# Four layers on one core: D u of two images added in a transfer, the last chunks of layer 3's first part shared out anew, and the order of the scans' first pair

## The chip, the cores and the metric

The kernel runs on one core of one Trainium2 chip. The metric is device time in microseconds (us). A core has five engines that work side by side, each through its own list of instructions in order: TensorE (PE, matmul, with its weight loads as PEld), VectorE (DVE), ScalarE (ACT), GpSimd (POOL) and SyncE (SP), which here only issues transfers. Sixteen DMA engines move data between DRAM and the on-chip memory. POOL and ACT can issue transfers too. An engine waits for another, or for a transfer, by a semaphore.

## The reference

Four layers follow each other on four images of 64 x 64 pixels and 128 channels: neighbourhood attention (layer 0), full attention over 4096 pixels with a group norm (layer 1), a gated pair update with a layer norm (layer 2), and a selective scan in four directions (layer 3). The change touches layer 3:

```python
xb, z = jnp.split(x @ Win, 2, axis=-1)            # 256 channels each
xb = silu(depthwise_conv_3x3(xb, conv_w) + conv_b)
xs = jnp.stack([xf, xf[..., ::-1], xt, xt[..., ::-1]], axis=1)
x_dbl = jnp.einsum('bcl,cd->bdl', xs_flat, Wxproj)  # dt (8 rows), B, C
dt_out = jnp.einsum('kdr,kbrl->bkdl', dt_weight, dt_kb)
delta = softplus(dt_out + dbias)
xc = exp(delta * A) * xc + delta * u * B            # the scan
y  = xc * C  +  u * Dv                              # D u
y = y0 + y1 + y2 + y3                               # directions turned back
out = (layernorm(y * silu(z))) @ Wout
```

The data of the four scan directions are regrouped by a reshape: direction k of the scan takes its delta, B and C from image k, and u of image k drives the scans that end in output b = 0 to 3. What concerns the change is that D u of image i must be added to the output of all images, forwards or backwards, and turned or not. The sum over directions is kept in DRAM, in two orders t = 0 (not turned) and t = 1 (turned).

## The kernel before

The images are handled one after another. For each image layer 0 runs in blocks of 128 pixels, then layer 1 in 32 query blocks. Beside layer 1 (`between(i)`, called after block i) run two further things: layer 2 of the same image, in eight chunks of 512 pixels with four steps each (`turn`, `mix`, `add`, `norm`), and layer 3's *first part* (`front(b)`, its function `turn(i)`). The first part of image b takes chunks 4 to 7 of image b - 1 and then chunks 0 to 3 of image b. For the last image nothing follows, so its chunks 4 to 7 are done at the end, by `end(i)`, for i from 30 to 42; attention's last block is over at about i = 33.

The first part does the following with a chunk n of image i:

- `load`, `project`: 128 x 512 inputs are multiplied with `win` into x for the convolution, in `xh` (one slot for even, one for odd chunks, each with a row above and one below, which are copied between neighbouring chunks by POOL, L785 and L786). The row below a chunk is known only when the next chunk is projected.
- `gate`: z's half, silu, stored in `zf_d`.
- the convolution with nine taps. In most chunks ACT makes the first product (`begin`), ACT and POOL do four taps (`multiply`, `add_parts`: `gsum`, `tp`), and DVE four (`add_taps`, L858). At the end, PE does it for chunks 5 and 6 of the last image (`convolve_by_pe`, L873), with nine matmuls by diagonal matrices for each half f of the 256 channels. Chunk 7 gives six taps to DVE and two to POOL (`taps`).
- `activate`: silu to u. `lower`: `pd` (x_dbl), written to `dbl_d`; B as a row for every partition (`pb` by PE in chunk 3 and at the end); D u; and u times B, stored in `ub_d`.

D u is handled in `lower` in two ways. Images 0 and 2 (even) scale u on ACT (L934) and store it once, in their own output's place of `y_d` (`sum_of`). Images 1 and 3 (odd) had `load_du` load what the image before stored (L898, SP), add their own by one DVE operation (L929, written reversed), and store the result to all four outputs (L931, SP). Each half of a chunk is 256 KB.

`layer_3` then runs the scans in 64 pairs of steps. A step is 1024 pixels of one half f, one image k and one output b. For each pair: `deltas` (PE `pdt`, ACT softplus `de` L1206, POOL `inp` = de times u B, L1210), `decay` (ACT exp to `h`, L1220, in two PSUM buffers), `back` (DVE scan L1234, then times C into `yo`, L1248), and POOL issues a transfer that adds `yo` to `y_d` (L1249). `deltas` of the next pair is written ahead of `decay` of the present one. Softplus and exp need different tables on ACT. The scans use u B of half f = 0 for the first four pairs (`early.ub`, loaded ahead), then of f = 1 (`load_ub`, L1145, issued by SP in front of the first pair). A last part adds the turned sums, multiplies by the gate, norms and projects.

The order of instructions on an engine is not that of the program's text: a list scheduler at build time places them, except that instructions passed to `keep_in_program_order` keep theirs. SP's queue is such an ordered list as well; a transfer in it that has to wait holds up all behind it.

Of the kernel before, what the change touches and what calls it, by code (L numbers as in the profile page):

```python
# [22 lines left out]
F32 = mybir.dt.float32  # L23
AF = mybir.ActivationFunctionType
ALU = mybir.AluOpType
# [4 lines left out]
P = 128  # L30
B, H, W, C = 4, 64, 64, 128
L = H * W
NT = L // P
BR, BC = 8, 16
CH = 512
# [103 lines left out]
def layers_0_to_2(  # L139
# [15 lines left out]
    def ps_o(shape, name):  # L155
        return psp.tile(shape, F32, name=name, tag="o", bufs=2)
# [594 lines left out]
    def by_image_rows(t):  # L751
        return t.rearrange("p (i j) -> p i j", j=W)

    def front(b):
# [33 lines left out]
        def project_row(i, n):  # L788

# [34 lines left out]
        def taps(i, n):  # L824


            v = (1, 0) if n < NCH - 1 else (-1, 0)
            gp, ve = [v, (-1, 1), (1, -1), (1, 1)], [(-v[0], 0), (0, -1), (0, 1), (-1, -1)]
            return (gp[:2], ve + gp[2:]) if (i, n) == (B - 1, NCH - 1) else (gp, ve)

        def multiply(i, n, f, which):
            for k in which:
# [31 lines left out]
                for t in range(9):  # L864
                    nc.gpsimd.tensor_scalar(dg[:, f, t, :], ident, cc[:, f, t:t + 1], None, ALU.mult)

        def convolve_by_pe(i, n, f):
            ps = ps_o([P, CH], "pc3")
            sums.setdefault(n, []).append(ps)
            order = [(0, 0)] + [(dy, dx) for dy in (-1, 0, 1) for dx in (-1, 0, 1) if (dy, dx) != (0, 0)]  # L870
            for k, (dy, dx) in enumerate(order):
                r0, r1, c0, c1 = region(n, dy, dx)
                nc.tensor.matmul(  # L873
                    by_image_rows(ps)[:, r0:r1, c0:c1], lhsT=x_of["dg"][:, f, 3 * (dy + 1) + dx + 1, :],
                    rhs=xh[:, n & 1, f, 1 + r0 + dy:1 + r1 + dy, c0 + dx:c1 + dx], start=(k == 0), stop=(k == 8),
                )

        def activate(i, n, apart=False):
            if apart:
                u_of[i, n] = [tmp.tile([P, CH], F32, name="u1", tag="c512", bufs=9) for _ in range(2)]  # L880
                for f in range(2):
                    if (i, n) in ((B - 1, 5), (B - 1, 6)):
                        nc.scalar.activation(u_of[i, n][f], sums[n][f], AF.Silu, bias=cl("conv_b", f))
# [11 lines left out]
        def load_du(i, n):  # L895
            for f in range(2):
                z = x_of[i, n, "z", f] = tmp.tile([P, CH], F32, name="du", tag="c512", bufs=9)
                nc.sync.dma_start(z, sum_of(i, n, f, i - 1))  # L898

        def lower(i, n):  # L900


            lo, hi = CH * n, CH * n + CH
            u = u_of[i, n]
            pd = ps_t([P, P], "pd")
            for f in range(2):
                for g in range(4):
                    nc.tensor.matmul(
                        pd[HD * g:HD * g + HD, :], lhsT=wx[:, f, :], rhs=u[f][:, bass.ts(g, P)],
                        start=(f == 0), stop=(f == 1),  # L910
                    )
            dq = tmp.tile([P, P], F32, name="dq", tag="gb")
            nc.scalar.copy(dq, pd)
            for g in range(4):
                nc.sync.dma_start(dbl_d[i][:, lo + P * g:lo + P * g + P], dq[HD * g:HD * g + NDBL, :])
            if by_product(i, n):
                pb = ps_s([P, CH], "pb3")
                for g in range(4):
                    r = HD * g + RANK
# [73 lines left out]
        def end(i):  # L993

            c = B - 1
            for n, at in ((5, 30), (6, 34), (7, 38)):
                if i == at:
                    load(c, n)
                    project(c, n)
                if i == at + (4 if n == 6 else 1):  # L1000
                    gate(c, n)
            if i in (30, 31):
                convolve(c, 4, range(2), i - 30)
            if i in (35, 36):
                convolve_by_pe(c, 5, i - 35)
            if i == 38:
                convolve_by_pe(c, 6, 0)
                convolve_by_pe(c, 6, 1)
            if i == 38:
                convolve(c, 7, range(2), 0)  # L1010
                convolve(c, 7, range(2), 1)
            for n, at in ((4, 35), (5, 37), (6, 39), (7, 39)):
                if i == at - 1:
                    load_du(c, n)
                if i == at:
                    activate(c, n, True)
                if i == at + 1:
                    lower(c, n)
            if i == NT:

                early.ub = big.tile([P, L], F32, name="ub_0", tag="qT")
                early.dbl, early.cb = ring([P, L], "dbl"), ring([P, L], "cb_0")
                for k in range(2):
                    nc.sync.dma_start(early.dbl[32 * k:32 * k + NDBL, :], dbl_d[k])
                for g in range(2):
                    nc.sync.dma_start(early.ub[:, bass.ts(g, L // 2)], ub_d[0][0][:, bass.ts(g, L // 2)])
                nc.sync.dma_start(early.cb, dbl_d[0][RANK + 1:RANK + 2, :][0].partition_broadcast(P))

        def turn(i):
# [8 lines left out]
            if j < 8:  # L1038
# [9 lines left out]
                if r == 3:  # L1048
                    for c in takes[j]:
                        gate(*c)  # L1050
                    for c in takes[j + 1] if j < 7 else []:
                        load(*c)

            for c, at in zip(whole, u_at):
                if c and i == at - 1 and c[0] & 1:
                    load_du(*c)
# [55 lines left out]
def layer_3(ctx, tc, of, dt, na, ident, cl, big, early, x3_d, ub_d, zf_d, y_d, dbl_d, ct_d, gw_d, bw_d):  # L1112
# [56 lines left out]
    with pool("s", 2) as sp, pool("psC", 2, space=PSUM) as psp:  # L1169
# [43 lines left out]
                parts.append((de, inp))  # L1213
            return parts

        def decay(step, de):

            f, k = step[0:2]
            h = psp.tile([P, SC], F32, name="h", tag="h")
            act(nc.scalar.activation(h, de, AF.Exp, scale=na[:, 2 * k + f:2 * k + f + 1]))  # L1220
            return h

# [260 lines left out]
```

## Time and profile before

| | us |
|---|---|
| median of 3 runs | 3831.19 |
| lowest, highest | 3826.19, 3833.25 |
| the profiled execution | 3828.72 |
| span of it in the trace | 3826.9 |
| attention of image 1, busy PE in 1000:1700 | 661.97 of 700 |
| attention's last matmul (L640) ends | 3121.4 |
| first scan (L1234) starts | 3200.6 |
| last scan starts | 3656.8 |

| engine | busy us | share |
|---|---|---|
| PE | 3401.1 | 89% |
| DVE | 2829.9 | 74% |
| ACT | 2681.4 | 70% |
| POOL | 1420.2 | 37% |

The kernel has stages with different limits, so shares over the whole span say little. Read a stretch: where one engine is full, only its work counts; where none is, look for who waits for whom. A line of the timeline gives the start, the length, the engine, the line of the code, what is written from what, the number of merged instructions, and in brackets how long the engine sat idle before it and what ended that. "SPq" is an issue on SP's queue.

### The profile page before, as it was taken

Reading aid. Unit: us, or ns where it says so; the run is one execution under the profiler, and the core shown is the slowest. Engines: PE = TensorE matmul, PEld = TensorE weight load, DVE = VectorE, ACT = ScalarE, POOL = GpSimd, SP = SyncE. Lnnn points to the kernel's source line nnn. Section 1 sums busy time; section 2 is a strip of 40 time slices with the busy share of each in tenths; the row PEclk is TensorE's granted clock in tenths of the full one; section 3 lists DMA queues with packets and bytes.
Section 4 is the critical chain, followed back from the end, with each engine's and each line's share of the span. In section 5 each row is a group of like instructions: output and inputs, shape, how many; then the busy total and the mean of one; then the engine's idle time right before and its main releaser. Section 6 shows DMA issues by size and latency. Waiting matters only on the chain.

```text
span 3826.9 us, 69375 instructions
## 1 busy us (share of the span) xinstructions
PE 3401.1 (89%) x26780; PEld 2787.6 (73%) x26780; DVE 2829.9 (74%) x4865; ACT 2681.4 (70%) x4350; POOL 1420.2 (37%) x1562
## 2 busy tenths in 40 slices
PE   6999999999899999998999999989999987666647
PEld 4679989966799889667998897669888863222236
DVE  3657777756677788666787886667877866999968
ACT  3865667778676776686766776866767756999934
POOL 5510012245122122352122223522221326999866
PEclk8999999999999999999999999999999996555579
DMA  5100000131010012310211112100101148999998
GB/s 141 47 3 25 12 18 29 43 99 35 18 42 32 32 62 82 121 43 1 74 66 48 51 52 94 46 1 23 41 31 59 57 166 220 232 220 204 213 276 280
DMA packets 205199, 319.30 MB, mean 83 GB/s; under 512 B 23583, under 2 KB 112188, under 8 KB 200732
## 3 DMA queue, kind: packets, MB, share of 16 engines
q1 hardware_dynamic: 165572, 237.57, 18.2%
q0 software_dynamic: 19776, 68.56, 9.8%
q10 hardware_dynamic: 19520, 8.73, 0.8%
q8 instruction: 211, 3.46, 0.4%
q14 instruction: 120, 0.98, 0.1%
HBM read 150.91 MB, written 155.56 MB: 80 GB/s over the span
## 4 chain that ended last, share of the span: by engine, by line
PE 49%; DVE 24%; ACT 9%; POOL 8%; issue 6%; DMA 2%; SPq 1%; POOLq 0%; ACTq 0%; DVEq 0%
PE po L640 15%; PE sc L607 14%; POOL inp L1210 4%; DVE mx L619 4%; DVE acc L858 3%; DVE st L633 3%; POOL y L1249 3%; PE pt L491 3%; DVE mx L614 3%; PE sc L456 2%; PE po L502 2%; ACT st L634 2%; ACT pr L474 2%; ACT st L610 2%; PE pz L808 1%
## 5 line engine op out<-in xcount | busy, mean ns | idle before, releaser
L640 PE MATMUL po<-v,st 128*128 128x129 f32 x8192 | 1081.3, 275 | 4.1 <-ACT st L634 4.1
L607 PE MATMUL sc<-qT,kT 128*128 128x128 f32 x8192 | 1081.9, 276 | 0.4 <-ACT st L610 0.4
L607 PEld LDWEIGHTS sc<-qT,kT 128*128 128x128 f32 x8192 | 1003.5, 193 | 21.9 <-issue 18.1
L640 PEld LDWEIGHTS po<-v,st 128*128 128x128 f32 x8192 | 998.8, 192 | 5.4 <-issue 5.4
L610 ACT COPY st<-sc 128x512 f32<-128x512 f32 x1024 | 577.8, 583 | 527.0 <-PE sc L607 519.6
L633 DVE TENSOR_TENSOR st<-st,pb 128x2048 f32<-128x2048 f32 x256 | 573.9, 2283 | 47.7 <-PE pb L630 47.1
L614 DVE TENSOR_TENSOR mx<-mx,st 128x1024 f32<-128x1024 f32 x256 | 315.3, 1232 | 239.3 <-ACT st L610 237.4
L634 ACT ACTIVATE st<-st 128x2048 f32<-128x2048 f32 x256 | 483.4, 1908 | 6.4 <-DVE st L633 4.7
L1199 PE MATMUL pdt<-dbl,dt 8*128 8x512 f32 x512 | 309.0, 1082 | 142.4 <-ACT de L1206 142.0
L1210 POOL TENSOR_TENSOR inp<-de,ub 128x1024 f32<-128x1024 f32 x128 | 412.1, 4479 | 36.0 <-ACT de L1206 29.0
L1199 PEld LDWEIGHTS pdt<-dbl,dt 8*128 8x128 f32 x512 | 114.4, 312 | 334.1 <-ACT de L1206 270.7
L704 POOL TENSOR_TENSOR x<-x,row 128x512 f32<-128x512 f32 x32 | 49.9, 1559 | 788.9 <-PE pt L274 788.9
L482 POOL TENSOR_SCALAR pr<-pr,sm 128x308 f32<-128x308 f32 (+3 forms) x512 | 243.5, 494 | 259.8 <-DVE sm L480 187.6
L849 POOL TENSOR_TENSOR gsum<-gsum,tp 128x504 f32<-128x504 f32 (+1 forms) x176 | 254.1, 1446 | 122.7 <-ACT gsum L837 83.9
L474 ACT ACTIVATE pr<-pr,mx 128x308 f32<-128x308 f32 (+3 forms) x512 | 262.5, 517 | 0.0
L619 DVE TENSOR_TENSOR mx<-mx 128x512 f32<-128x512 f32 (+2 forms) x384 | 256.9, 669 | 6.1
L1234 DVE TENSOR_TENSOR_SCAN h<-h,end,inp 128x1024 f32<-128x1024 f32 x96 | 221.1, 2346 | 14.7 <-POOL inp L1210 7.0
L491 PE MATMUL pt<-ident,pr 128*88 128x128 f32 (+5 forms) x1472 | 204.1, 276 | 7.8 <-ACT prT L493 7.8
L1249 POOL DMA_DIRECT2D y<-yo x112 | 206.5, 2823 | 7.3 <-DVE yo L1248 3.8
L460 DVE CUSTOM_DVE_ANT_0 pr<-sc,bias_m 128x266 f32<-128x266 f32 (+1 forms) x384 | 151.7, 451 | 69.6 <-PE sc L456 64.7
L858 DVE SCALAR_TENSOR_TENSOR acc<-xh,cc,acc 128x512 f32<-128x512 f32 (+3 forms) x244 | 196.4, 832 | 3.8 <-ACT acc L822 2.7
L491 PEld LDWEIGHTS pt<-ident,pr 128*88 128x88 f32 (+5 forms) x1472 | 163.6, 138 | 45.4 <-ACT prT L493 31.6
(233 smaller groups left out, 5254.7 us busy)
## 6 DMA issues: line engine op xcount, KB each, us to landing
y<-yo POOLq DMA_DIRECT2D x112, 512.0 KB, 10.4
y<-du SPq DMA_DIRECT2D x160, 256.0 KB
zf_d<-zf SPq DMA_DIRECT2D x64, 256.0 KB
ub_d<-u SPq DMA_DIRECT2D x64, 256.0 KB
ub<-ub_d SPq DMA_DIRECT2D x16, 1024.0 KB
yl<-y SPq DMA_DIRECT2D x64, 256.0 KB
zc<-zf_d SPq DMA_DIRECT2D x64, 256.0 KB
x<-in_x SPq DMA_DIRECT2D x128, 64.0 KB
```

The costliest lines, as they stand in the source:

```text
L474: pin(nc.scalar.activation(k.pr[:, h], k.pr[:, h], AF.Exp, bias=k.mx[:, h:h + 1], accum_out=k.sm[:, h:h + 1]))
L491: pin(nc.tensor.transpose(pt[0:n, h, :], k.pr[:, h, at:at + n], ident))
L607: nc.tensor.matmul(ps[:, r, :], lhsT=kT[:, bass.ts(G * g + r, P)], rhs=qT[:, bass.ts(i, P)], start=True, stop=True)
L610: nc.scalar.copy(k.st[:, G * g:G * g + G, :], ps)
L614: nc.vector.tensor_tensor(k.mx, k.mx, k.st[:, 4 * g - 4:4 * g + 4, :], ALU.max)
L619: nc.vector.tensor_tensor(mx[:, 0:n, :], mx[:, 0:n, :], mx[:, n:2 * n, :], ALU.max)
L633: nc.vector.tensor_tensor(part, part, pb.unsqueeze(1).to_broadcast([P, 16, P]), ALU.add)
L634: nc.scalar.activation(part, part, AF.Exp)
L640: nc.tensor.matmul(k.po, lhsT=k.st[:, j, :], rhs=v[:, j, :], start=(j == 0), stop=(j == NT - 1))
L1199: nc.tensor.matmul(pdt[j][:, g, :], lhsT=dt[o:o + RANK, P * f:P * f + P], rhs=at(dbl[o:o + RANK, :], k & 2, g0, g0 + CH), start=True, stop ...
L1210: nc.gpsimd.tensor_tensor(by_rows(inp), by_rows(de), at(ub_s[f], b ^ (k & 1), SC * n, SC * n + SC), ALU.mult)
L1249: nc.gpsimd.dma_start(here if f == 1 and k == 3 else there, yo, accum_op=ALU.add)
```

## The change

Seven edits:

- `lower`: odd images now also scale u on ACT, written reversed, and POOL issues a transfer that adds it to the place where the even image before stored its own. `load_du` and the DVE operation are gone.
- `copy_du`: six transfers of 512 KB for each pair of chunks, from that place in DRAM to the other three outputs in DRAM, both halves, issued by SP. They come some blocks later (i = 16, 28, 32, and i = 8 of the next image); for the last image's chunks 2 to 7 at i = 40 in the text.
- `taps`, `end`, `activate`: of the last image chunk 5 goes to DVE, ACT and POOL with chunk 7's split; chunk 6 stays with PE; of chunk 7 half f = 0 goes to PE and half f = 1 stays.
- `convolve_by_pe`: may be called in two parts: part 0 leaves out the chunk's last row of the taps from below, part 1 does that row alone, after the next chunk's projection. The first matmul of a call is kept in program order.
- `project`: the row copies of the last image's chunks 6 and 7 are DVE's.
- `end`: new places for load, project, gate, activate and lower of chunks 4 to 7.
- `layer_3`: the first pair's exponentials stand ahead of the second pair's `deltas`; their PSUM buffers are taken first.

```diff
+            row = nc.vector if at_end(i, n) and n > 5 else nc.gpsimd
...
-                nc.gpsimd.tensor_copy(xh[:, me, :, 0, :], xh[:, 1 - me, :, RC, :])
-                nc.gpsimd.tensor_copy(xh[:, 1 - me, :, RC + 1, :], xh[:, me, :, 1, :])
+                row.tensor_copy(xh[:, me, :, 0, :], xh[:, 1 - me, :, RC, :])
+                row.tensor_copy(xh[:, 1 - me, :, RC + 1, :], xh[:, me, :, 1, :])
...
-            return (gp[:2], ve + gp[2:]) if (i, n) == (B - 1, NCH - 1) else (gp, ve)
+            return (gp[:2], ve + gp[2:]) if i == B - 1 and n in (5, 7) else (gp, ve)
...
-        def convolve_by_pe(i, n, f):
+        def convolve_by_pe(i, n, f, part=None):
+            if part != 1:
+                sums[n, f] = ps_o([P, CH], "pc3")
+            ps = sums[n, f]
+            order = [(dy, dx) for dy in (-1, 0, 1) for dx in (-1, 0, 1) if (dy, dx) != (0, 0)]
+            order = order[5:] if part == 1 else [(0, 0)] + order
             for k, (dy, dx) in enumerate(order):
                 r0, r1, c0, c1 = region(n, dy, dx)
+                if dy == 1 and part is not None:
+                    r0, r1 = (RC - 1, RC) if part else (0, RC - 1)
...
+        def copy_du(i, n):
+            m = (L - CH * (n + 2)) // SC
             for f in range(2):
-                z = x_of[i, n, "z", f] = tmp.tile([P, CH], F32, name="du", tag="c512", bufs=9)
-                nc.sync.dma_start(z, sum_of(i, n, f, i - 1))
+                for b2 in range(B):
+                    if b2 != i - 1:
+                        nc.sync.dma_start(y_d[(i ^ b2) >> 1][b2][f][m], y_d[(i ^ (i - 1)) >> 1][i - 1][f][m])
...
             for f in range(2):
+                du = tmp.tile([P, CH], F32, name="du", tag="c512", bufs=9)
+                nc.scalar.activation(du[:, ::-1] if i & 1 else du, u[f], AF.Copy, scale=cl("d", 2 * i + f))
                 if i & 1:
-                    du = x_of.pop((i, n, "z", f))
-                    nc.vector.scalar_tensor_tensor(du, u[f][:, ::-1], cl("d", 2 * i + f), du, ALU.mult, ALU.add)
-                    for b2 in range(B):
-                        nc.sync.dma_start(sum_of(i, n, f, b2), du)
+                    nc.gpsimd.dma_start(sum_of(i, n, f, i - 1), du, accum_op=ALU.add)
                 else:
-                    du = tmp.tile([P, CH], F32, name="du", tag="c512", bufs=9)
-                    nc.scalar.activation(du, u[f], AF.Copy, scale=cl("d", 2 * i + f))
                     nc.sync.dma_start(sum_of(i, n, f, i), du)
...
+            if i in (30, 34, 38):
+                n = i // 4 - 2
+                load(c, n)
+                project(c, n)
+            if i == 31:
+                gate(c, 5)
             if i in (30, 31):
                 convolve(c, 4, range(2), i - 30)
+            if i == 34:
+                convolve(c, 5, range(2), 0)
+                convolve(c, 5, range(2), 1)
+                activate(c, 4, True)
             if i in (35, 36):
-                convolve_by_pe(c, 5, i - 35)
+                convolve_by_pe(c, 6, i - 35, 0)
+            if i == 36:
+                lower(c, 4)
+                activate(c, 5, True)
+            if i == 37:
+                lower(c, 5)
+                gate(c, 6)
             if i == 38:
+                convolve(c, 7, (1,), 0)
+                convolve(c, 7, (1,), 1)
+                for f in range(2):
+                    convolve_by_pe(c, 6, f, 1)
+                activate(c, 6, True)
+                convolve_by_pe(c, 7, 0)
+                lower(c, 6)
+                gate(c, 7)
+            if i == 39:
+                activate(c, 7, True)
+            if i == 40:
+                lower(c, 7)
+                for n in (2, 4, 6):
+                    copy_du(c, n)
...
+            for k, at in ((0, 16), (2, 28), (4, 32)):
+                if i == at and whole[k] and whole[k][0] & 1:
+                    copy_du(*whole[k])
+            if b > 0 and i == 8 and (b - 1) & 1:
+                copy_du(b - 1, 2)
...
+        hs = [states() for _ in range(2)]
         parts = deltas(todo[0][1])
+        hs = [decay(step, de, h) for step, (de, _), h in zip(todo[0][1], parts, hs)]
...
             coming = deltas(after[1]) if after else None
-            hs = [decay(step, de) for step, (de, _) in zip(pair, parts)]
+            if j > 0:
+                hs = [decay(step, de) for step, (de, _) in zip(pair, parts)]
```

In `activate`, the chunks read from PE's sums are now (6, both halves) and (7, f = 0) instead of chunks 5 and 6. `states` takes a PSUM buffer that `decay` took before.

More of the change, by code (lines that the diff above doesn't have):

```diff
@@ L865, in diagonals @@
                     nc.gpsimd.tensor_scalar(dg[:, f, t, :], ident, cc[:, f, t:t + 1], None, ALU.mult)
-        def convolve_by_pe(i, n, f):
-            ps = ps_o([P, CH], "pc3")
-            sums.setdefault(n, []).append(ps)
-            order = [(0, 0)] + [(dy, dx) for dy in (-1, 0, 1) for dx in (-1, 0, 1) if (dy, dx) != (0, 0)]
+        def convolve_by_pe(i, n, f, part=None):
[4 more added lines that the diff above has]
+            order = order[5:] if part == 1 else [(0, 0)] + order
             for k, (dy, dx) in enumerate(order):
                 r0, r1, c0, c1 = region(n, dy, dx)
-                nc.tensor.matmul(
+                if dy == 1 and part is not None:
+                    r0, r1 = (RC - 1, RC) if part else (0, RC - 1)
+                ins = nc.tensor.matmul(
                     by_image_rows(ps)[:, r0:r1, c0:c1], lhsT=x_of["dg"][:, f, 3 * (dy + 1) + dx + 1, :],
-                    rhs=xh[:, n & 1, f, 1 + r0 + dy:1 + r1 + dy, c0 + dx:c1 + dx], start=(k == 0), stop=(k == 8),
-                )
+                    rhs=xh[:, n & 1, f, 1 + r0 + dy:1 + r1 + dy, c0 + dx:c1 + dx], start=(k == 0 and part != 1),
+                    stop=(k == len(order) - 1 and part != 0),
+                )
+                if k == 0:
+                    tc.keep_in_program_order(ins)
         def activate(i, n, apart=False):
@@ L881, in activate @@
                 for f in range(2):
-                    if (i, n) in ((B - 1, 5), (B - 1, 6)):
-                        nc.scalar.activation(u_of[i, n][f], sums[n][f], AF.Silu, bias=cl("conv_b", f))
+                    if i == B - 1 and (n, f) in ((6, 0), (6, 1), (7, 0)):
+                        nc.scalar.activation(u_of[i, n][f], sums.pop((n, f)), AF.Silu, bias=cl("conv_b", f))
                     else:
@@ L893, in sum_of @@
             return y_d[(i ^ b) >> 1][b][f][at // SC][:, at % SC:at % SC + CH]
-        def load_du(i, n):
+        def copy_du(i, n):
+            m = (L - CH * (n + 2)) // SC
             for f in range(2):
-                z = x_of[i, n, "z", f] = tmp.tile([P, CH], F32, name="du", tag="c512", bufs=9)
-                nc.sync.dma_start(z, sum_of(i, n, f, i - 1))
+                for b2 in range(B):
+                    if b2 != i - 1:
+                        nc.sync.dma_start(y_d[(i ^ b2) >> 1][b2][f][m], y_d[(i ^ (i - 1)) >> 1][i - 1][f][m])
         def lower(i, n):
@@ L995, in end @@
             c = B - 1
[L996 to L1001, printed above, removed]
+            if i in (30, 34, 38):
[4 more added lines that the diff above has]
+                gate(c, 5)
             if i in (30, 31):
                 convolve(c, 4, range(2), i - 30)
+            if i == 34:
+                convolve(c, 5, range(2), 0)
+                convolve(c, 5, range(2), 1)
+                activate(c, 4, True)
             if i in (35, 36):
-                convolve_by_pe(c, 5, i - 35)
-            if i == 38:
[L1007 to L1018, printed above, removed]
+                convolve_by_pe(c, 6, i - 35, 0)
[5 more added lines that the diff above has]
+                gate(c, 6)
+            if i == 38:
+                convolve(c, 7, (1,), 0)
[12 more added lines that the diff above has]
+                    copy_du(c, n)
             if i == NT:
@@ L1052, in turn @@
                         load(*c)
+            for k, at in ((0, 16), (2, 28), (4, 32)):
[3 more added lines that the diff above has]
+                copy_du(b - 1, 2)
             for c, at in zip(whole, u_at):
-                if c and i == at - 1 and c[0] & 1:
-                    load_du(*c)
                 if c and i == at:
@@ L1214, in deltas, with states, decay @@
             return parts
-        def decay(step, de):
+        def states():
+            return psp.tile([P, SC], F32, name="h", tag="h")
+        def decay(step, de, h=None):
             f, k = step[0:2]
-            h = psp.tile([P, SC], F32, name="h", tag="h")
+            h = states() if h is None else h
             act(nc.scalar.activation(h, de, AF.Exp, scale=na[:, 2 * k + f:2 * k + f + 1]))
```

## The prediction

> **What bounds the kernel now.** I read the busy table by stretches first, then the timeline of the stretch in which no engine is full, then the starts of one instruction that comes once per query block of layer 1. The attention stretches are held by TensorE (662 of 700 us busy in 1000:1700), with VectorE close behind where layer 3's first part is interleaved. The scans, 3201 on, run at about 7.0 us per pair of steps, VectorE and ScalarE both full. Between lies a passage without a full engine:
>
> ```profile
> 3107.00:3122.00 15.00, 15.00 (x136) 14.88 (x135) 8.78 (x21) 9.98 (x10) 2.51 (x2) 1.00 0.40 129
> 3122.00:3150.00 28.00, 26.58 (x114) 13.51 (x113) 11.83 (x27) 8.27 (x12) 2.87 (x4) 1.00 0.77 269
> 3150.00:3176.00 26.00, 20.58 (x56) 8.62 (x55) 9.06 (x14) 8.80 (x14) 7.71 (x5) 0.87 0.83 302
> 3176.00:3201.00 25.00, 20.68 (x84) 9.94 (x84) 7.17 (x12) 12.46 (x16) 2.48 (x2) 0.70 0.81 274
> 3201.00:3300.00 99.00, 67.35 (x114) 25.29 (x112) 97.22 (x79) 96.94 (x85) 98.62 (x59) 0.50 0.93 198
> ```
>
> Columns: PE, PE loads, DVE, ACT, POOL, clock, DMA share, GB/s. Attention's last matmul ends at 3121; the first scan starts 80 us later. In it PE is the busiest, but in order behind waits. The timeline shows what is in line:
>
> ```profile
> 3122.17 5.26 PE L873 MATMUL pc<-xh,dg 128*128 128x512 f32 x12
> 3127.93 1.12 PE L873 MATMUL pc<-xh,dg 128*128 128x512 f32 x2
> 3133.45 9.50 PE L873 MATMUL pc<-xh,dg 128*128 128x504 f32 x22
> 3156.85 18.22 PE L873 MATMUL pc<-xh,dg 128*128 128x512 f32 x36 [5.06 <-ACT u L883]
> 3186.95 1.12 PE L1199 MATMUL pdt<-dbl,dt 8*128 8x512 f32 x2
> 3190.95 2.12 ACT L1206 ACTIVATE de<-pdt,col 128x1024 f32<-128x1024 f32 x2
> 3195.21 1.55 SPq L942 DMA_DIRECT2D ub_d<-u  x2
> 3200.86 9.26 POOL L1210 TENSOR_TENSOR inp<-de,ub 128x1024 f32<-128x1024 f32 x4 [6.38 <-DMA ub_d<-u]
> 3207.96 4.60 DVE L1234 TENSOR_TENSOR_SCAN h<-h,end,inp 128x1024 f32<-128x1024 f32 x2
> ```
>
> Chunk 5's convolution (the first 36 records, 15.9 us; a record is half a matmul) stands before chunk 7's layer 2; chunk 6's (18.2 us) comes only after chunk 7's projection, as it needs that chunk's first row. Then five small steps, the first softplus (3190.95), and a POOL multiply that waits for the store of the last u, which SP issues behind eight stores of D u.
>
> In the attention, the cost of an odd image's D u can be read by comparing blocks. `L626` starts once per block:
>
> ```profile
> 1382.04 0.29 DVE L626 TENSOR_REDUCE nm<-pt 128x1 f32<-128x128 f32 x1 [0.42 <-PE pt L624]
> 1542.60 0.29 DVE L626 TENSOR_REDUCE nm<-pt 128x1 f32<-128x128 f32 x1
> 2162.09 0.29 DVE L626 TENSOR_REDUCE nm<-pt 128x1 f32<-128x128 f32 x1 [0.42 <-PE pt L624]
> 2317.47 0.28 DVE L626 TENSOR_REDUCE nm<-pt 128x1 f32<-128x128 f32 x1
> ```
>
> The same nine blocks take 160.56 us in image 1, whose own chunks are odd, and 155.38 in image 2, whose are even.
>
> [...] every accumulating issue is on POOLq. [...] SP stands still before each copy until the sum has landed. No row of before shows a copy within DRAM. [...] For 512 KB [...] the trace has 5.1 at least and 10.4 in the median (`y<-yo`), so for 256 KB I take 5 us from issue to landing, bounds 3 and 10. [...]
>
> **The change, part by part.** The changed program's instruction order gives the rest.
>
> *1. D u in the attention.* Removed: per odd chunk two VectorE operations of 0.75 us (L929), two loads and eight stores of 256 KB. Added: two ScalarE scalings (0.71 us, the row that even images have, L934), two POOL issues (0.86 to 2.6 us, from L1249), later copies. In the new order the blocks of image 2's first half stand on PE, DVE and ACT exactly as image 1's do in both programs, and image 1's second half as image 0's but for one place. So measured even blocks price odd ones:
> - image 1, 23rd to 32nd block: 160.56 - 155.38 = 5.2 us;
> - image 2, 4th to 23rd (odd there, even in image 1): 349.85 (1812.24 to 2162.09) - 348.50 (1033.54 to 1382.04) = 1.35 us;
> - image 3, 23rd to 29th: 112.37 (2935.59 to 3047.96) - 110.62 (2162.09 to 2272.71) = 1.75 us;
> - image 3's last such chunk: two times 0.72 us in 3084:3106, where DVE is busy 21.2 of 22 us: 1.4 us.
>
> Sum 9.7 us. POOL's issues and ScalarE's 22 us lie beside PE (POOL busy 90, ACT 245 of 350 us in 2600:2950). The copies, 30 of them before attention ends for the last time, meet a DMA share of 0.17 to 0.18 (1000:1700, 1800:2500); the set ahead of image 2's loads of v leaves these some 18 us (issued from 1570.5, first used at 1593.5, less the 3 us of five issues). If that cover is gone, some 2 us each at three places.
>
> *2. Chunks shared out anew.* Chunk 5 goes to DVE, ACT and POOL: 12 taps, 8.5 us on a DVE that is busy 12 of 28. Chunk 6's part without its last row takes chunk 5's place on PE; after chunk 7's projection there remain six one-row matmuls (about 1.6 us, at 0.13 us a record from short transposes) and nine of chunk 7. I follow PE's new order from 3121.2. Transposes, chunk 3's two small steps, chunk 6's projection, chunk 7's layer 2 products: to 3129. Nine matmuls of chunk 6 (0.87 each): 3136.8. Chunk 7's py waits for POOL's multiply (L700), behind DVE's twelve taps and one POOL issue: 3139.6, against 3142.8 now. Nine more: 3148.4; then chunk 4's product, the transposes, chunk 5's steps and chunk 6's gate, so chunk 7's projection ends at 3156.1, 4.3 us later than now (3151.8). Copies and a row: 0.6 + 0.6 + 0.3; six short ones: 3159.1; nine at the slower clock of that stretch (1.01 each, from 18.22/18): 3168.2, against 3175.1. The row copies that move from POOL to DVE (0.3 us each) free L700 of a wait for PE; that is counted in the 3139.6.
>
> *3. The last chunks' end.* Now 11.9 us from the convolution's end to `pdt`; chunk 5's product and a wait for a late silu fall away, chunks 6 and 7 keep theirs: 8.2 us, `pdt` at 3176.4. Gain 10.5.
>
> *4. First pair.* The exponential of pair 0 now comes before pair 1's softplus. It brings the first scan forward, but pair 1's exponential still needs pair 2's softplus ahead of it, and that needs matmuls of 4.78 us that start only when pair 1's is read. Softplus starts 4.0 us after `pdt` (as now): 3180.4. Pair 1's scan now comes 17.0 us after that (3207.96 - 3190.95), then 16.6: 4.6 to the first exponential, 1.1 and 1.3 of it and a table, 1.1 + 4.8 + about 1 for pair 2's softplus to start, then 1.1, 1.3, 1.1 and waits. So 3197.0: gain 11.0. POOL waits for the first yo before its third multiply; it still delivers at about 3196.
>
> *5. Transfers at the seam.* The store of the last u is issued right after its product (3177), lands by 3182 (4.1 us as now), and chunk 7's sum, issued at 3174.5 to 3177, by 3182: both before the scan needs inp. Then SP waits for that landing, issues six copies (3.1 MB) and only then ub of the other half (2.1 MB), needed by pair 4's multiply at 3211. Copies at the trace's best rate (314 GB/s) take 10 us, at half of it 20. With 7.5 us for ub and 2 for landing, from 3186: 3205.5 to 3215.5. I take 3206, hidden; the upper end costs 4.5.
>
> **Sum.** 9.7 + 11.0 = 20.7. The profiled execution (3826.9 span, 3828.72 in all) would be 3808.0; it lies 2.5 below the median, so 3810.5.
>
> **Rivals.**
> *A, one of the two gains is missing.* Either tail path is eaten by chunk 7's later projection (for: 4.3 us later already, and my chain of steps is long; against: nine fewer matmuls behind it), or the scans take back what starts earlier. Price: about -10, 3821.
> *B, no change.* Both gains are small: odd blocks cost the same on ScalarE, whose tp waits show up elsewhere, and the seam moves by under 4 us: 3828.
> *C, slower: copies.* If copies within DRAM run slowly, SP's queue holds ub back behind the last six: pair 4 stalls POOL, DVE and ACT alike. It cancels all gains when ub lands 20.7 us after 3211, and is slower by 0.2% (7.7 us; about what can be told from no change) at 28 us: six copies in 43 us, under 73 GB/s. At 60 GB/s: 52 us, ub at 3248, a stall of 37, 3847. For: DMA share 0.8 to 0.9 at the seam, no row of such copies. Against: 302 GB/s there now, and fewer bytes in all (40 MB of loads and stores go, 8 of sums and 24 of copies come).
>
> **Numbers.** Forecast 0.60 (3804 to 3816); A 0.22 (3816 to 3824); B 0.11; C 0.07. Range for 8 in 10: 3801, where the tail gains 4 more than worked out and attention somewhat more, to 3822. Faster by over 0.2%: all of the forecast and nearly all of A, 0.81; within: 0.12; slower 0.07.
>
> **What would show it.** Right: image 1's nine blocks at about 155.4; `pdt` 55 us after attention's last matmul instead of 66; pair 1's scan 76 after it instead of 87; the scans' length unchanged. Wrong: odd blocks unchanged (step 1); the six short matmuls start later than 37 us after attention (step 2); POOL's first multiply waiting for a sum, or the ninth for ub (step 5).

## The result, and the profile after

| | before | after |
|---|---|---|
| median, us | 3831.84 (4 runs) | 3808.74 (4 runs) |
| lowest, highest | 3826.19, 3833.25 | 3805.62, 3812.28 |
| ratio, 95% interval | | 0.9943 (0.9926 to 0.996) |
| profiled execution, span | 3826.9 | 3810.5 |
| attention's last matmul ends | 3121.4 | 3115.4 |
| from there: chunk 7's `py` (L711) | 21.4 | 19.3 |
| end of PE's last convolution | 53.7 | 49.2 |
| first `pdt` | 65.6 | 56.7 |
| pair 0's scan, pair 1's scan | 79.2, 86.6 | 66.0, 75.4 |
| pair 1's scan to the last scan | 448.9 | 450.2 |

The change is faster by 0.57%, some 22 us. The profiled execution after is the slowest of its four runs, so the two spans differ by 16.4 only: 6.0 in attention, 11.2 between attention and pair 1's scan, less 1.3 in the scans, and 0.5 behind them. The second profile of the changed kernel, taken below, has 8.0 and 11.0 in the first two places.

The stretches of after, the first three moved with attention's end and the last with the first scan; columns PE, PE loads, DVE, ACT, POOL, clock, DMA share, GB/s:

```profile
3101.00:3116.00 15.00, 15.00 (x136) 14.90 (x134) 8.76 (x21) 10.04 (x11) 4.31 (x4) 1.00 0.49 120
3116.00:3144.00 28.00, 23.00 (x96) 11.90 (x95) 17.21 (x34) 15.53 (x24) 13.57 (x12) 0.94 0.95 275
3144.00:3170.00 26.00, 21.98 (x113) 11.75 (x111) 9.96 (x15) 10.42 (x18) 4.30 (x4) 0.93 0.90 266
3184.00:3283.00 99.00, 69.60 (x119) 26.09 (x115) 95.27 (x78) 95.31 (x83) 95.53 (x58) 0.50 1.00 228
```

Behind attention DVE has 17.2 us of work instead of 11.8 (chunk 5's taps), PE 23.0 instead of 26.6, and the DMA engines are busy for 0.95 of the time instead of 0.77, at hardly more GB/s (275 against 269). The timeline of after, the lines that answer to those shown before:

```profile
3122.51 7.49 PE L879 MATMUL pc<-xh,dg 128*128 128x512 f32 x18
3129.63 1.28 ACT L695 ACT_TABLE_LOAD   x1 [5.31 <-DMA y<-du]
3131.65 0.75 DVE L699 SCALAR_TENSOR_TENSOR o<-pl,b_le,sg 128x512 f32<-128x512 f32 x1 [1.09 <-DMA ub_d<-u]
3134.71 1.70 PE L711 MATMUL py<-ma,o 128*128 128x128 f32 x8 [4.14 <-POOL o L700]
3136.20 8.67 PE L879 MATMUL pc<-xh,dg 128*128 128x512 f32 x18
3152.91 1.55 PE L879 MATMUL pc<-xh,dg 128*128 128x63 f32 x12 [1.16 <-DVE xh L787]
3155.28 9.29 PE L879 MATMUL pc<-xh,dg 128*128 128x512 f32 x18 [0.82 <-ACT u L893]
3172.10 1.99 PE L1225 MATMUL pdt<-dbl,dt 8*128 8x512 f32 x8
3174.11 2.12 ACT L1232 ACTIVATE de<-pdt,col 128x1024 f32<-128x1024 f32 x2 [1.24 <-PE pdt L1225]
3190.75 4.66 DVE L1263 TENSOR_TENSOR_SCAN h<-h,end,inp 128x1024 f32<-128x1024 f32 x2 [2.39 <-POOL inp L1236]
```

PE's work stands as the prediction followed it: nine matmuls of chunk 6, `py`, nine more, six short ones, nine of chunk 7. `py` starts 1.1 us later than predicted, about as much as VectorE waits (1.09 us) ahead of L699, behind chunk 5's taps. Two things were missing until then: a buffer, which a store of `ub_d` freed, and ACT's gate `sg` (L695), which was ready at the same moment, since ACT waited 5.31 us until a sum of D u had landed and freed a buffer. In the attention, the block starts that bound image 1's nine blocks:

```profile
1382.66 0.29 DVE L626 TENSOR_REDUCE nm<-pt 128x1 f32<-128x128 f32 x1 [0.42 <-PE pt L624]
1538.71 0.28 DVE L626 TENSOR_REDUCE nm<-pt 128x1 f32<-128x128 f32 x1
```

They take 156.05 us, 4.5 less than before (in the second profile 154.8).

### The profile page after: what moved, and what is told of

It is laid out like the page before. It is cut to its first block, busy times and chain, and to the rows that moved or that the text cites. A ratio compares the mean times of both kernels' runs of the same rounds, so it can differ in the third digit from the quotient of the medians.

```text
span 3810.5 us, 69239 instructions
## 1 busy us (share of the span) xinstructions
PE 3389.1 (89%) x26774; PEld 2780.3 (73%) x26774; DVE 2805.3 (74%) x4843; ACT 2702.5 (71%) x4385; POOL 1445.8 (38%) x1592
## 3 DMA queue, kind: packets, MB, share of 16 engines
q1 hardware_dynamic: 144068, 220.79, 17.1%
## 4 chain that ended last, share of the span: by engine, by line
PE 47%; DVE 25%; ACT 10%; POOL 7%; issue 7%; DMA 3%; SPq 1%; POOLq 0%; DVEq 0%; ACTq 0%
PE po L640 14%; PE sc L607 14%; DVE mx L619 4%; POOL inp L1236 4%; DVE acc L859 4%; DVE st L633 3%; PE pt L491 3%; DVE mx L614 2%; POOL y L1278 2%; ACT st L634 2%; PE sc L456 2%; PE po L502 2%; ACT st L610 2%; ACT pr L474 2%; PE pz L809 1%
## 5 line engine op out<-in xcount | busy, mean ns | idle before, releaser
L1236 POOL TENSOR_TENSOR inp<-de,ub 128x1024 f32<-128x1024 f32 x128 | 412.3, 4463 | 10.3 <-DMA ub_d<-u 6.2
```

The lines of the kernel that those rows point to most:

```text
L1236: nc.gpsimd.tensor_tensor(by_rows(inp), by_rows(de), at(ub_s[f], b ^ (k & 1), SC * n, SC * n + SC), ALU.mult)
```

## The experiments

All ratios are against the kernel before on the same chip, with the 95% interval. "Stretch" is the time from the end of attention's last matmul to the start of pair 1's scan, in the profile.

### The parts apart

`du_only`: the kernel before, with these parts of the change alone (and the copies of chunks 2 to 7 at i = 40).

```diff
+            for k, at in ((0, 16), (2, 28), (4, 32)):
+                if i == at and whole[k] and whole[k][0] & 1:
+                    copy_du(*whole[k])
...
+                nc.scalar.activation(du[:, ::-1] if i & 1 else du, u[f], AF.Copy, scale=cl("d", 2 * i + f))
                 if i & 1:
+                    nc.gpsimd.dma_start(sum_of(i, n, f, i - 1), du, accum_op=ALU.add)
```

> The kernel before with only the new handling of D u (scaling on ScalarE, sum in a transfer, copies within DRAM); the last chunks' shares, their order in end() and the scans' first pair are as before. Theory (the two gains are separate and add up): attention's last matmul ends 6 to 10 us earlier than in the kernel before and the stretch from there to the second pair's scan stays at 84 to 87 us, so 7 to 11 us faster in all. Rival (the new D u makes most of the gain at the end too, by taking the eight stores per chunk out of SP's queue and two operations per chunk from VectorE): that stretch shrinks to under 80 us and the kernel is 15 us faster or more.

`tail_only`: the kernel after, with the old `load_du`, VectorE operation and four stores.

```diff
-                nc.scalar.activation(du[:, ::-1] if i & 1 else du, u[f], AF.Copy, scale=cl("d", 2 * i + f))
+                    du = x_of.pop((i, n, "z", f))
+                    nc.vector.scalar_tensor_tensor(du, u[f][:, ::-1], cl("d", 2 * i + f), du, ALU.mult, ALU.add)
```

> The changed kernel with the old handling of D u (two loads, one VectorE operation per half, four stores per half), so only the new shares of the last chunks, the new end() and the first pair's order remain of the change. Theory (separate gains): attention ends as in the kernel before (within 1 us), the stretch from its last matmul to the second pair's scan is 75 to 79 us instead of 87, the kernel 8 to 12 us faster. Rival (the shares help only once D u is off SP's and VectorE's queues): that stretch stays above 82 us and the kernel gains under 5 us.

`no_first_pair`: the kernel after, without the last edit.

```diff
-        hs = [decay(step, de, h) for step, (de, _), h in zip(todo[0][1], parts, hs)]
...
-            if j > 0:
-                hs = [decay(step, de) for step, (de, _) in zip(pair, parts)]
+            hs = [decay(step, de) for step, (de, _) in zip(pair, parts)]
```

> The changed kernel with the exponentials of the scans' first pair back behind the second pair's deltas. Theory (the first pair's order brings only the first scan forward, the second pair's scan being held by the chain softplus, table, exponential or by GpSimd's multiply): first scan 4 to 9 us later, second pair's scan within 1 us, kernel within 1 us of the changed one, so 20 to 23 us faster than before. Rival (the order is worth its face value): second pair's scan and the end 4 us later or more, so 18 us faster than before or less.

> The changed kernel unaltered, beside the others on one chip. Theory (in the block of image 3 that takes 22.04 us where the kernel before takes 17.45, one 128x128 VectorE operation of layer 2's norm takes 5.31 us rather than 0.34[...]): the same operation of that block is again over 4 us long, as the instruction order decides it. Rival (chance): the operation takes under 1.5 us this time and the block 17 to 18 us, and the profiled run is 4 us nearer to the unprofiled median.

| | median | ratio | attention ends | stretch |
|---|---|---|---|---|
| du_only | 3811.04 | 0.9941 (0.9928 to 0.9954) | 3114.9 | 71.6 |
| tail_only | 3829.73 | 1.0002 (0.9994 to 1.0011) | 3124.8 | 85.3 |
| no_first_pair | 3809.99 | 0.9946 (0.9934 to 0.9959) | 3108.8 | 76.1 |
| after_again | 3809.99 | 0.9945 (0.9933 to 0.9958) | 3113.3 | 75.6 |

The theory of two separate gains falls. D u alone brings all of the gain, at the end too, and shortens the stretch by 15.0 us, more than the whole change does (11.2). The new shares and the first pair's order alone bring nothing. That attention ends 3.5 us later in `tail_only` than in before, against the expectation, is mostly scatter between executions: 2.8 us of it are there when attention of image 1 starts. The four profiles with the old D u in the attention end it between 3120.5 and 3124.8. In the timeline of `tail_only`:

```profile
3130.43 0.75 DVE L939 SCALAR_TENSOR_TENSOR du<-u,col,du 128x512 f32<-128x512 f32 x1 [4.31 <-DMA du<-y]
...
3139.42 0.60 PE L689 MATMUL pr<-rs,ma 128*128 128x8 f32 x2 [9.25 <-DVE rs L683]
```

The old D u waits on DVE for its load, chunk 5's taps stand behind it, and among them the small reduction L683 on which PE's whole queue then waits 9.25 us. The first pair's order brings the first scan 2.9 us forward (69.2 to 66.25) and pair 1's by 0.5. That is less than the 4 to 9 us expected for the first scan, and as expected nothing for the kernel: both medians are 3809.99.

### What of D u shortens the end

`du_tail`: the kernel before, with the new D u in image 3's chunks 4 to 7 only.

```diff
+                if i & 1 and at_end(i, n):
+                    du = tmp.tile([P, CH], F32, name="du", tag="c512", bufs=9)
+                    nc.scalar.activation(du[:, ::-1], u[f], AF.Copy, scale=cl("d", 2 * i + f))
+                    nc.gpsimd.dma_start(sum_of(i, n, f, i - 1), du, accum_op=ALU.add)
-                if i & 1:
+                elif i & 1:
```

> The kernel before with the new handling of D u in image 3's chunks 4 to 7 alone (the four that run after attention); all other odd chunks keep loads, VectorE operation and four stores. The theory of the prediction (shares and D u gain apart) has fallen with the first runs; new theory (most of the gain at the end is D u leaving VectorE's and SP's queues there): attention's last matmul ends within 1.5 us of the kernel before, the stretch from it to the second pair's scan is 71 to 76 us instead of 87, kernel 11 to 16 us faster. Rival (what shortens the end is set up in attention, by all odd chunks together): that stretch stays above 80 us and the kernel gains under 7 us.

`du_dve_copy`: the kernel before, with one store instead of four there, and the same copies at the end.

```diff
-                    for b2 in range(B):
+                    for b2 in (i - 1,) if at_end(i, n) else range(B):
```

> The kernel before with one thing changed in image 3's chunks 4 to 7: load and VectorE operation stay, but of the four stores per half only one is made, and the other three outputs get theirs by copies within DRAM at the end. Theory (the VectorE operation that stands in an in-order queue and waits for its loads is what costs): the stretch from attention's last matmul to the second pair's scan stays at 82 to 88 us, kernel within 4 us of before. Rival (the 32 stores in SP's queue are what costs): the stretch falls under 78 us, kernel 9 us faster or more.

`du_tail` has a ratio of 0.9966 (0.9952 to 0.9979) and a median of 3816.44; attention ends at 3122.0 and the stretch is 72.7 us. The four chunks' D u is 13.9 us of the stretch, the odd chunks in the attention have no part in it. `du_dve_copy` has 0.9988 (0.9981 to 0.9994), 3825.95, its stretch is 80.8: between theory and rival. By subtraction, one store with copies instead of four stores is worth 5.8 us, and the rest (no loads, no VectorE operations, but a scaling on ACT and a sum) the other 8.1.

Most of it lies at chunk 6's convolution: in `du_tail` it ends 43.4 us after attention instead of 53.7, which is 10.3 of the 13.9; the other 3.6 come behind it. Before, this convolution waits 5.06 us for the silu of chunk 5 that frees PE's sums, and takes 18.22 us for 36 records. ACT's queue up to that silu, in the timeline of before:

```profile
3144.48 0.27 ACT L913 COPY dq<-pd 128x128 f32<-128x128 f32 x1 [7.21 <-PE pd L908]
3150.97 0.58 ACT L781 COPY xh<-pi 128x512 f32<-128x512 f32 x1 [4.62 <-PE pi L780]
3154.81 1.28 ACT L883 ACT_TABLE_LOAD   x1
3156.11 1.26 ACT L883 ACTIVATE u<-pc,col 128x512 f32<-128x512 f32 x2
```

And in the timeline of `du_tail`:

```profile
3134.04 3.56 PE L873 MATMUL pc<-xh,dg 128*128 128x504 f32 x8
3137.44 1.16 PE L711 MATMUL py<-ma,o 128*128 128x128 f32 x8
3139.00 0.67 ACT L883 ACTIVATE u<-pc,col 128x512 f32<-128x512 f32 x1
3145.54 1.87 PE L873 MATMUL pc<-xh,dg 128*128 128x512 f32 x4
3151.57 13.75 PE L873 MATMUL pc<-xh,dg 128*128 128x512 f32 x32
```

The silu (L883) starts 17.1 us after attention's end instead of 34.8, `py` 15.5 instead of 21.4, and the convolution has no wait. What differs is the order of instructions. Before, the silu has no wait of its own: it stands in ACT's queue behind instructions that wait 7.21 and 4.62 us for PE, and on PE `py` stands behind the last 22 records of chunk 5's convolution. In `du_tail` the scheduler put the silu ahead of those ACT instructions and `py` behind 8 of the records. So by the trace this wait is not one for the loads or stores of D u while the kernel runs; it came with the order that the scheduler chose at build time around them. In `du_dve_copy` the silu stands behind two instead of six instructions that follow chunk 7's projection, and PE still waited 2.66 us.

Why the scheduler chose so is open. `u`, `du`, `zf`, `sg` and others share nine buffers, and an old `du` keeps one from its load until four stores have landed; that would fit both runs, but no run tried it by itself, and none has the old D u with the new order. One direct wait for a store of the old kernel does go: GpSimd's second multiply of the scans waits 1.04 us instead of 6.38.

Part of the gain is the clock. The stretches with the convolution, of before:

```profile
3153.00:3161.00 8.00, 4.15 (x5) 1.85 (x6) 7.93 (x14) 6.53 (x10) 2.23 (x2) 0.65 0.97 320
3161.00:3169.00 8.00, 8.00 (x19) 3.49 (x18) 0.56 (x1) 0.00 (x0) 5.41 (x4) 0.92 1.01 394
```

and of `du_tail`:

```profile
3151.00:3159.00 8.00, 8.00 (x20) 3.61 (x19) 6.44 (x7) 6.16 (x10) 4.91 (x5) 1.00 0.98 348
3159.00:3167.00 8.00, 7.61 (x37) 3.56 (x36) 4.37 (x6) 0.27 (x1) 3.00 (x3) 1.00 0.94 244
```

Around and behind the wait of 5.06 us the granted clock (third column from the end) is 0.65 and 0.92; without it, it is 1.00. At its lowest, in before:

```profile
3156.00:3162.00 6.00, 5.15 (x6) 2.19 (x7) 5.57 (x9) 3.55 (x7) 2.97 (x1) 0.50 1.06 385
```

The convolution's 36 records take 18.22 us before and 1.87 + 13.75 = 15.62 here: 2.6 us, half of the wait again. In `du_dve_copy`, behind its wait of 2.66 us, they take 17.25. Why the clock falls there, and how long a wait has to be for it, was not shown.

### The block of image 3 that became longer

In after, image 3's 29th block takes 22.04 us (3037.41 to 3059.45) instead of 17.45. VectorE and GpSimd there, in the timeline of after:

```profile
3038.28 1.76 POOL L943 DMA_DIRECT2D y<-du  x2
3038.31 5.57 DVE L728 TENSOR_SCALAR x<-x,mv,rd 128x128 f32<-128x128 f32 x2
3039.44 3.14 POOL L951 TENSOR_TENSOR u<-u,bb 128x512 f32<-128x512 f32 x2
3041.92 1.87 POOL L850 TENSOR_TENSOR gsum<-gsum,tp 128x504 f32<-128x504 f32 x1
```

Two operations of layer 2's norm take 5.57 us where two take 0.60 elsewhere; the second of them, 5.31 us long, ends 0.1 us after GpSimd's row of five instructions. Over the whole trace of after, the 84 of these 128 operations that overlap no GpSimd instruction take at most 0.35 us each, the 44 that overlap one take 1.02 us on average; in before it is 88 of at most 0.35 us and 40 of 1.20. Why an operation takes longer beside GpSimd, no run shows. `after_again` shows 5.30 at the same place; `no_first_pair`, with the same order there, does not:

```profile
3038.24 0.60 DVE L728 TENSOR_SCALAR x<-x,mv,rd 128x128 f32<-128x128 f32 x2
```

Of the six profiles with the new D u in all odd chunks and the norm on VectorE, four show it and two don't (`no_first_pair`, `more_copies`, with blocks of 17.1). So it is neither the order alone nor a rare accident. In `no_first_pair` as in after the second operation starts 0.29 us behind the first issue, so what decides is finer than that. To take VectorE's part of the meeting away, the norm was moved, first to GpSimd, then to ScalarE.

```diff
-                nc.vector.tensor_scalar(x, x, mv[:, k, 0:1], rd[:, k:k + 1], ALU.subtract, ALU.mult)
+                nc.gpsimd.tensor_scalar(x, x, mv[:, k, 0:1], rd[:, k:k + 1], ALU.subtract, ALU.mult)
```

> The changed kernel with layer 2's norm (128 operations of 128x128 with two scalars per partition, L728) moved from VectorE to GpSimd. Theory (these operations cost 1.2 us, once 5.3, wherever GpSimd is at work[...]): VectorE's busy time falls by 65 us or more, no block of image 3 from the 29th on takes more than 21 us, attention ends 4 to 10 us earlier than in the changed kernel, the kernel is 4 to 10 us faster than the changed one, 24 to 30 faster than before. Rival (GpSimd's own queue holds them back, TensorE's transposes wait): attention ends later than in the changed kernel and the gain on before is under 20 us.

```diff
+            nc.vector.scalar_tensor_tensor(nb, mv[:, :, 0], -1.0, rd, ALU.mult, ALU.mult)
...
-                nc.vector.tensor_scalar(x, x, mv[:, k, 0:1], rd[:, k:k + 1], ALU.subtract, ALU.mult)
+                nc.scalar.activation(x, x, AF.Identity, bias=nb[:, k:k + 1], scale=rd[:, k:k + 1])
```

> The changed kernel with the same norm on ScalarE (scale and bias per partition; one small VectorE operation per chunk makes the bias). [...] as with GpSimd, 4 to 10 us faster than the changed kernel, as ScalarE is busy only 245 of 350 us in the attention. Rival (ScalarE's copies of scores, which TensorE waits for, come later by the 128 operations): no gain on the changed kernel or a loss of 1 to 5 us.

On GpSimd: 3801.47, 0.9926 (0.9914 to 0.9939), attention ends at 3103.9. On ScalarE: 3798.91, 0.9917 (0.9903 to 0.993), 3101.1. The medians lie some 8 and 11 us below the changed kernel's; with GpSimd its interval overlaps those of the changed kernel's two runs, with ScalarE it lies below that of `after_again`. VectorE's busy time falls by 22 us with GpSimd, not by 65 as expected: L728's 67.9 us are gone, but the maximum L612 rose from 162.2 to 201.5 (1267 to 1574 ns each). In after, the 8 of its 128 operations that overlap a GpSimd instruction take 2.01 us on average, the other 120 at most 1.23; that more of them overlap one with the norm on GpSimd is an estimate from these numbers. With ScalarE L612 stays at 162.1, and the busy time falls by 43, as the small operations for the bias take 18.5. The 29th block takes 18.9 and 17.4 us. These two runs don't tell what running beside GpSimd costs from plain load: the 128 operations also take 128 x 0.34 = 43.5 us of VectorE's time when nothing is in their way.

### The seam, and the row copies

`more_copies`: the kernel after, and on SP's queue ahead of the load of u B:

```diff
+                for q in range(12):
+                    spare = dram.tile([P, SC], F32, name=f"spare{q}")
+                    nc.sync.dma_start(spare, y_d[0][2][q & 1][0])
```

> The changed kernel with twelve more copies of 512 KB within DRAM (into places that nothing reads) behind the last six on SP's queue, so ahead of the load of u B for the fifth pair of scans. Theory (the seam's cover: the load is hidden by some 12 us; copies move at about the 290 GB/s of that stretch, so 6.3 MB take 22 us, and issuing them 9 us): the fifth pair's scan comes 4 to 16 us later against the second pair's than in the changed kernel (21.2 us), the kernel is slower than the changed one by as much. Rival C of the prediction (copies run at 60 to 75 GB/s): 40 us or more. Rival (there is cover for all of it): within 2 us.

3824.26, 0.9987 (0.9979 to 0.9995), 14 to 16 us slower than the changed kernel's medians. The fifth pair's scan stands 30.2 us behind pair 1's instead of 21.2; by the sixth pair the delay is 10.8, at the last scan 13.6. GpSimd's multiply for the fifth pair:

```profile
3215.05 2.33 POOL L1239 TENSOR_TENSOR inp<-de,ub 128x1024 f32<-128x1024 f32 x1 [4.77 <-DMA ub<-ub_d]
```

At the 310 GB/s of that stretch 6.3 MB are 20 us. They cost 9.0 at this pair, so by this estimate the six copies of the change have some 11 us of cover to spare. At rival C's rates of 60 to 75 GB/s the twelve would take over 80 us; that doesn't occur.

`row_pool`: the kernel after, with the row copies on GpSimd.

```diff
-            row = nc.vector if at_end(i, n) and n > 5 else nc.gpsimd
+            row = nc.gpsimd
```

> The changed kernel with the row copies of the last image's chunks 6 and 7 back on GpSimd. Theory of the prediction (the row copy waits for TensorE's convolution and holds GpSimd's multiply L700, for which chunk 7's layer 2 product waits): that product (L711) starts 2 to 4 us later after attention's end than 19.3 us, the second pair's scan 1 to 4 us later. Rival (GpSimd's multiply stands ahead of the copy anyway, or another wait takes over): both within 1 us.

3807.35, 0.9945 (0.9933 to 0.9958). `py` starts 19.3 us after attention in both, the stretch is 76.3: the edit is worth 0.9 us at most, and the wait for PE that the prediction meant to spare L700 doesn't show in it.

### Put together

`du_norm_act` is `du_only` with the norm on ScalarE, `du_norm_act_pair` has the first pair's order as well; both edits are shown above.

> The kernel before with the new handling of D u in all odd chunks and layer 2's norm on ScalarE; shares of the last chunks, their order and the first pair as before. Theory (with D u out of the way the new shares of the last chunks cost rather than gain: second pair's scan 71.6 us after attention's last matmul without them, 75.4 to 76.1 with them): 4 to 8 us faster than the changed kernel with the norm on ScalarE (3798.9), so 3791 to 3795. Rival (the shares gain once attention is the same): not faster than 3798.9, the stretch at 76 us or more.

> The same kernel with the new order of the scans' first pair added. Theory (the order is worth 0 to 1 us, since GpSimd's and ScalarE's chains hold the second pair): within 1.5 us of the run without it. Rival: 3 us or more faster.

| | median | ratio | attention ends | stretch |
|---|---|---|---|---|
| norm_act | 3798.91 | 0.9917 (0.9903 to 0.993) | 3101.1 | 79.2 |
| du_norm_act | 3793.37 | 0.9909 (0.9895 to 0.9922) | 3099.8 | 71.8 |
| du_norm_act_pair | 3795.70 | 0.9916 (0.9902 to 0.9929) | 3100.3 | 74.2 |

`du_norm_act` has the lowest median of all, 0.91% faster than before. That the new shares cost something shows in the stretch: with the first pair's order alike on both sides, 5.0 us here (79.2 against 74.2) and 4.5 in the kernels with the norm on VectorE (`no_first_pair` against `du_only`). In the times it is not shown, as the intervals of the three rows overlap. The first pair's order costs 2.5 us of stretch in this kernel and gains 0.5 to 0.7 in the changed one; the median is 2.3 us higher with it, outside the 1.5 expected, within the intervals.

## Why the number was right, and the reason was not

*Step 1, D u in the attention (9.7).* The mechanism held; the profiled ends moved by 6.0 and 8.0, in the two profiles without the long operation by 9.5 (`more_copies`) and 12.5 (`no_first_pair`), with a scatter of some 4 us between executions. The terms are off both ways. Image 1's nine blocks gave 4.5 (5.8 in `after_again`) for 5.2. Image 2's blocks up to the 23rd (from 1812.24, which is the third block's start, not the 4th's) gave 4.3 instead of 1.35: I took an even block with the same instructions as the price, but in it L728 runs beside GpSimd too. Its 16 operations there fell from 11.75 us to 8.34, below the 11.2 of the blocks of image 1 that served as the price. Image 3's 23rd to 29th gave 3.5 instead of 1.75, and the 29th then lost 4.6. What "POOL's issues ... lie beside PE" left out is VectorE: two such issues stand in the row beside which L728 took 5.31 us.

*Steps 2 and 3, the end (10.5).* PE's walk came out as written, a little late: `py` at 19.3 after attention (18.2 predicted), chunk 7's projection done at 36.4 (34.8), six short matmuls at 37.5 (36.2 worked out; "later than 37" was the sign of being wrong for step 2, and it came by half a microsecond), convolution's end at 49.2 (46.8), then 7.5 to `pdt` (8.2), which stood at 56.7 (55.1). The term that was mis-sized is the landing of a sum: I took 5 us, with 10 as the bound, an estimate from the 5.1 us at least and 10.4 in the median that sums of 512 KB took in before; at the end six of twelve took 10.7 to 12.6, and one of these held ACT's gate. But both steps credit the shares with the gain. The step that failed is step 2's comparison, the convolution's end at "3168.2, against 3175.1": it takes the 3175.1 of before as what stands without the shares, and D u of these four chunks has no term in it. I priced that at nothing, because I looked at its operations and not at the order that comes with its loads and stores. With the new D u and the old shares the convolution ends 43.3 us after attention (`du_only`), and the shares move that to 49.2. Step 3's term held: from there to `pdt` it is 10.0 us in `du_only` and 7.5 with the shares, which makes good 2.5 of the 5.9 lost. So that 11.0 came out as 11.2 is luck: another part of the change earned it.

*Step 4, first pair (11.0 in sum).* 75.4 against 75.7. The softplus came 2.0 us after `pdt` instead of 4.0, as the eight matmul records took 1.99 us, and pair 1's scan 16.6 after it, as predicted (a table load between softplus and exponential takes 1.28 us); the 2.0 us made good for `pdt`'s 1.6 of delay. The scan was released by GpSimd's multiply. It stands behind an issue that waits for `yo`, and it ended 0.1 us after the exponential on which the predicted 16.6 was built:

```profile
3187.47 0.88 POOL L1278 DMA_DIRECT2D y<-yo  x1 [3.80 <-DVE yo L1277]
```

*Step 5, the seam (nothing).* Right, with some 11 us to spare by the estimate above. Before did have transfers within DRAM from which to price the copies: its 16 adding ones (`y<-y`, 512 KB) landed in 5.8 us at the median. The 2 us that the prediction gives a landing there were an estimate; in before the shortest medians from issue to landing are 1.9 us (`t_d<-in_rpb`, 1.4 KB) and 2.1 (`be<-t_d`, 33.2 KB). SP did wait for the sums: those of chunk 7 landed at 3174.98 and 3177.52, the first copy of each half was issued at 3175.00 and 3177.54, and the load of u B behind them at 3180.16.

Rival A, "one of the two gains is missing", named the right weakness, chunk 7's later projection: that is where the shares lose. The total hid it, since D u gave more than both steps asked.

## What to carry to other kernels

When a change has several parts, a sum that fits does not say which part earned it; build each part alone. Taking work away changes more than its busy time: a scheduler at build time will place everything else anew, so compare the engines' orders before and after, and look for what stood in line. Look at the longest, not the median, of short VectorE operations that run beside GpSimd: L728's was 5.31 us in after, at a median of 0.34.

## What was not expected of the hardware

- A VectorE operation of 0.34 us took 5.3 us while five GpSimd instructions, two of them issues of transfers, followed each other without a gap, in four of six profiles.
- Moving these operations to GpSimd lengthened another VectorE operation, L612, from 1267 to 1574 ns on average; moving them to ScalarE did not.
- Behind a PE wait of 5.06 us the granted clock was 0.50 (3156 to 3162), and the convolution behind it took 18.22 us, against 15.62 without the wait; behind a wait of 2.66 us it took 17.25.
- In after, sums of 256 KB landed in 3.7 to 12.6 us after their issue (median 5.5). The six that took over 10 us are all behind attention's end, where the DMA share is 0.9 and more.
